# Graph attention with residual GCN: repeated rows by one load, two chunks in one load, and stores spread over steps

## The chip, the core and the metric

The kernel runs on one core of one Trainium2 chip. The metric is the device time of one execution in microseconds. A core has a matrix engine (PE; its weight loads are shown as PEld), a vector engine (DVE), an activation engine (ACT), a general engine (POOL) and a sync engine (SP) that does no arithmetic here and issues nearly all transfers. Sixteen DMA engines move the data of all queues between the chip's memory (HBM) and the on-chip memory, whose 128 rows are called partitions.

## The reference

Inputs are `x` (2708 x 128), a weighted adjacency matrix `adj` (2708 x 2708) and the weights of two layers.

```python
# layer 0: attention, h = 8 features a head, d = 128 heads, n = m = 2708 nodes
q = (x @ Wq.T).reshape(d, n, h)            # k and v alike
a = einsum('dnh,dmh->dnm', q, k) * d**-0.5 + adj + adj
o = einsum('dnm,dmh->dnh', softmax(a, axis=2), v).reshape(n, h * d) @ Wo.T
x = layernorm(x + o)
# layer 1: two graph convolutions and a residual
hid = adj @ (x @ W2) + b2
x = layernorm(x + adj @ (hid @ W4) + b4 + hid @ res_w.T + res_b)
```

Nearly all time goes into `a`: 128 heads of 2708 x 2708 scores, each of which gets the same `adj` added (twice), is exponentiated and multiplied with eight features and a column of ones.

## The kernel before

**Heads and blocks.** The 128 heads go in 32 groups of GB = 4. The 2708 queries go in 6 blocks of QB = 452 (the last of 448). The 2708 keys are 21 whole chunks of 128 (NU = 21) and a short one of 20. A block is worked through in nine steps, the list `plan`; 32 x 6 x 9 gives 1728 steps. Each step has two to four pieces, and a piece is two score tiles of 128 keys by 452 queries. PE makes the scores (`score`, L451), DVE adds the adjacency tile (`add_near`, L458), ACT takes the exponential of a whole step's tiles at once (L559), and PE multiplies with the values into `acc` (`add_up`, L476). For nine of the chunks (`TWO_EXP`), three heads of four go another way: ACT takes the exponential of the bare scores (L556) and POOL multiplies by the exponential of the adjacency tile (L557), which was stored in the first group (`near_exp`).

**Precision.** Keys and queries are split in a rounded part and a remainder. `qs` and `ks` in HBM have 16 rows: eight of the rounded parts, eight of the remainders. A score needs (k + k')(q + q'), so each head holds 32 partitions on chip: the keys as 8 rounded rows twice and then 8 remainder rows twice, the queries as all 16 rows twice.

**Loads.** All of these are issued by SP from within the step that is being written down, and they stand in SP's queue in that order.

- `load_adj(n)` (L303) issues the nth entry of `loads`, the adjacency tiles in the order of their use; there are 26 entries a block. An ordinary chunk is one load of 128 x 452 into `col` (L316), the stored exponential one into `ecol` (L312), and a piece made of two different chunks has two loads into the halves of one tile `two` (L309). They are issued in the first piece of a step (c == 0), up to `ahead` = 8 entries past what the step needs. There are 9 buffers of `col`, 3 of `two`, 7 of `ecol`.
- `load_keys(g + 1, h)` (L261) runs for h = 0 to 15, one call in every second of a group's first 32 steps (t counts a group's 54 steps). One call loads 8 rows of 2708 numbers into 8 partitions of `k_raw`. Later steps rearrange them on POOL (`order_keys`).
- `load_q` (L295) runs in step 3 of a block for the next block: eight loads in a row, each of 16 rows of 452 numbers.
- `hand_on` (L479) runs once a block: DVE copies `acc` to `o`, and SP issues four stores of 9 rows in a row (L485).
- In the first 27 groups there are also the projections of later rows: quarter by quarter a load of weights, a product, and stores to `qs`, `ks`, `vs`, as jobs taken out one at a time in the second piece of a step (c == 1).

**What sets the order.** `interleave` writes down the order of pieces, products and `hand_on` by a table of costs; it does not look at loads. Each engine then runs its own instructions in that order and waits on semaphores. The semaphores of SP's transfers are eight, used in turn, so that a ninth transfer waits until the first has landed.

**Before the loop** (L383 to L419) the first two chunks of rows are projected, stored to `ks`, `qs` and `vs`, and read back by sixteen `load_keys` and eight loads of `load_q`, alternating between SP's and ACT's queues. **After the loop** `finish` does the output projection, the layer norm and layer 1; in the last group some of its first inputs are loaded early.

Of the kernel before, what the change touches and what calls it, by code (L numbers as in the profile page):

```python
# [9 lines left out]
F32 = mybir.dt.float32  # L10
F32R = mybir.dt.float32r
# [7 lines left out]
P = 128  # L19
H = 8  # L20
GB = 4
NB = 512
QB = 452
# [12 lines left out]
def chunks(n, w):  # L36
    return [(i, min(w, n - i)) for i in range(0, n, w)]
# [102 lines left out]


@with_exitstack
def graph_attention_gcn(ctx: ExitStack, tc: tile.TileContext, x, xT, adj, adjT, adjP, adjS,
                        WqT, WkT, WvT, WoT, W2, b2, W4, b4, res_wT, res_b, out):


# [7 lines left out]
    nc = tc.nc  # L154
    N, D = x.shape
    R = N * D
    NG = D // GB
    MC = chunks(N, P)
    NM = len(MC)
    NBS = chunks(N, NB)  # L160
    QBS = chunks(N, QB)


    NU = NM - 1
# [14 lines left out]
    qs = dram.tile([2 * H, R], F32, name="qs")  # L179
    ks = dram.tile([2 * H, R], F32, name="ks")  # L180
    vs = dram.tile([R, H], F32, name="vs")
    os_ = dram.tile([H + 1, R], F32, name="os")
# [19 lines left out]
    with ExitStack() as s:  # L202
# [3 lines left out]
        qpool = s.enter_context(tc.tile_pool(name="qpool", bufs=2))  # L206
# [52 lines left out]
        groups, raw_keys, values, queries, adj_cols, exp_cols, acc = {}, {}, {}, {}, {}, {}, {}  # L259

        def load_keys(g, h, queue=nc.sync):  # L261


            if h == 0:
                groups[g] = kpool.tile([P, NU, P], F32R, tag="k", name="k"), k_short[g % 2], vals[g % 2], v_short[g % 2]
                raw_keys[g] = raw.tile([P, N], F32R, tag="k_raw", name="k_raw")
            queue.dma_start(raw_keys[g][ds(H * h, H), :].bitcast(F32),
                              ks[ds(H * (h % 4 // 2), H), ds((GB * g + h // 4) * N, N)])

        def order_keys(g, i, copy=nc.gpsimd.tensor_copy):  # L270

# [9 lines left out]
        def load_values(g, j):  # L281
            if j == 0:
                values[g] = raw.tile([P, GB, NU * H], F32, tag="v_raw", name="v_raw")
            vz = v_short[g % 2]
            r0 = (GB * g + j) * N
            nc.sync.dma_start(values[g][:, j, :], vs[ds(r0, P * NU), :].rearrange("(p c) e -> p (c e)", c=NU))
            nc.sync.dma_start(vz[ds(32 * j, SHORT), ds(32 * j, H)], vs[ds(r0 + P * NU, SHORT), :])

        def spread_values(g, j):
            to = vals[g % 2].rearrange("p c (j e) -> p j c e", e=VW)  # L290
            v = values[g][:, j, :].rearrange("p (c e) -> p c e", e=H)
            nc.gpsimd.tensor_copy(to[:, j, :, :H], v)
            nc.gpsimd.tensor_copy(v_first[g % 2][:, ds(32 * j, H)], v[:, first_chunk, :])

        def load_q(g, b, queues=(nc.sync, nc.sync)):  # L295
            n0, nw = QBS[b]
            q = queries[g, b] = qpool.tile([P, QB], F32R, tag="q", name="q")
            for j in range(GB):
                for i in range(2):
                    queues[i].dma_start(q[ds(32 * j + 2 * H * i, 2 * H), :nw].bitcast(F32),  # L300
                                      qs[:, ds((GB * g + j) * N + n0, nw)])

        def load_adj(n):  # L303
            g, b, m = loads[n]
            n0, nw = QBS[b]
            if isinstance(m, tuple):
                t = adj_cols[g, b, m] = twos.tile([P, 2, QB], F32, tag="two", name="two")
                for i, x in enumerate(m):
                    nc.sync.dma_start(t[:, i, :nw], (adjS if x == NU else adjP[ds(x * P, P), :])[:, ds(n0, nw)])  # L309
            elif m < 0 and g > 0:  # L310
                t = exp_cols[g, b, -1 - m] = ecols.tile([P, QB], F32, tag="ecol", name="ecol")
                nc.sync.dma_start(t[:, :nw], near_exp[b, -1 - m][:, :nw])  # L312
            else:
                t = adj_cols[g, b, m] = cols.tile([P, QB], F32, tag="col", name="col")
                m = -1 - m if m < 0 else m
                nc.sync.dma_start(t[:, :nw], adjP[ds(m * P, P), ds(n0, nw)])  # L316

        ahead = 8
        epool = s.enter_context(tc.tile_pool(name="weights", bufs=5))
# [88 lines left out]
        for i in range(2):  # L408
            project_all(0, i)()
        store_v = project_all(0, 2)  # L410
        for h in range(16):
            load_keys(0, h, nc.scalar if h % 2 else nc.sync)
        load_q(0, 0, (nc.sync, nc.scalar))
        store_v()
        for n in range(2, ahead):
            load_adj(n)
# [62 lines left out]
        def hand_on(g, b):  # L479
            n0, nw = QBS[b]  # L480
            o = opool.tile([P, QB], F32, tag="o", name="o")
            nc.vector.tensor_copy(o[:, :nw], acc.pop((g, b))[:, :nw])  # L482
            queue = nc.gpsimd if (g, b) == (NG - 1, len(QBS) - 1) else nc.sync
            for j in range(GB):
                queue.dma_start(os_[:, ds((GB * g + j) * N + n0, nw)], o[ds(32 * j, H + 1), :nw])  # L485

        where = {}

# [2 lines left out]
        for g in range(1, NG):  # L491
            c = (min(NG, g + 2) * GB * N - 1) // (P * P)
            assert c < FIRST or amid[quarters.index((c, 2, 3))] + 8 < 54 * g
        jobs = []
        loaded = ahead
        for what, n, c, beside in interleave(plan, len(steps) // len(plan), NU, amid, bufs=5):
            if what == "amid":
                at = amid.index(n)
                jobs += project(at)
                continue  # L500
            if what == "add_up":
                g, b = divmod(n, len(QBS))
                add_up(g, b, c, where.pop((g, b, c)))
                continue
            if what == "hand_on":
                hand_on(*divmod(n, len(QBS)))
                continue
            g, b, i = steps[n]
            pieces, two, _ = plan[i]
            nw = QBS[b][1]  # L510
            if c == 1 and jobs:
                jobs.pop(0)()
            if c == 0:
                nq = (g, b + 1) if b + 1 < len(QBS) else (g + 1, 0)
                if i == 3 and nq[0] < NG:
                    load_q(*nq)

                if g + 1 < NG:
                    t = b * len(plan) + i
                    if t < 32 and t % 2 == 0:  # L520
                        load_keys(g + 1, t // 2)
                    elif t < 32 and t % 8 == 7:
                        load_values(g + 1, t // 8)
                    elif 33 <= t < 50 and t % 2:
                        order_keys(g + 1, (t - 33) // 2)
                    elif t >= 50:
                        spread_values(g + 1, t - 50)
                if g == NG - 1 and i % 2 and early:
                    nc.sync.dma_start(*early.pop(0))
                last = max(loads.index((g, b, x), max(0, loaded - 40)) for x in [chunks_of(p) for p in pieces] + [-1 - two])  # L530
                while loaded < min(len(loads), last + 1 + ahead):
                    load_adj(loaded)
                    loaded += 1
                e = epool.tile([P, 8, QB], F32, tag="e", name="e")
                sp = pq.tile([P, 3, NB], F32, tag="p", name="p")
                w = ppool.tile([P, 3, QB], F32, tag="w", name="w")
                if g == 0:
                    first_exp(b, two)
                at = k = 0
            st = ps.tile([P, 2, NB], F32, tag="s", name="s")  # L540
            for r, (m, j) in enumerate(pieces[c]):
                score(st[:, r], g, b, m, j)
                where.setdefault((g, b, m), {})[j] = e, at + r
            for j in beside:
                score(sp[:, k], g, b, two, j)
                where.setdefault((g, b, two), {})[j] = w, k
                k += 1
            add_near(e, st, g, b, pieces[c], at)
            at += 2
            if c == len(pieces) - 1:  # L550
                look_at_near(g, b, two)
                if n == len(steps) - 1:
                    quotient = opool.tile([P, QB], F32, tag="o", name="o")[:, :P]
                    nc.vector.reciprocal(quotient, ot0[:, H, :])
                    nc.vector.tensor_mul(ot0[:, :H, :], ot0[:, :H, :], quotient.unsqueeze(1).to_broadcast([P, H, P]))
                nc.scalar.activation(w[:, :, :nw], sp[:, :, :nw], AF.Exp, scale=2.0)  # L556
                nc.gpsimd.tensor_mul(w[:, :, :nw], w[:, :, :nw],  # L557
                                     exp_cols[g, b, two][:, :nw].unsqueeze(1).to_broadcast([P, 3, nw]))
                nc.scalar.activation(e[:, :at, :nw], e[:, :at, :nw], AF.Exp, scale=2.0)  # L559
# [538 lines left out]
```

## Time and profile before

| what | value |
|---|---|
| median of the runs | 6857.9 us |
| range of the runs | 6836.81 to 6862.31 us |
| time of the profiled execution | 6849.71 us |
| its span | 6847.9 us |
| ACT busy | 6504.6 us (95%) |
| PE busy | 6633.7 us (97%) |
| DVE busy | 6117.5 us (89%) |
| POOL busy | 5791.3 us (85%) |
| DMA, mean busy share of 16 engines, SP's queue | 79.7% |
| moved | 1665.68 MB, 243 GB/s |

The shares are means over the whole span. The loop over steps runs from about 46 us to about 6536 us; the rest is the start and `finish`. A row of the window view gives each engine's busy time in one stretch, the number of its instructions, the granted clock, the DMA share and the rate. In a group's row the last part is idle time of the engine just before these instructions, and what ended most of it.

### The profile page before, as it was taken

To read this page: it belongs to the slowest core of one execution; us is meant where nothing else is said; L and a number is where in the kernel's file an instruction comes from. 1 tells how busy PE (TensorE), PEld (TensorE's weight loads), DVE (VectorE), ACT (ScalarE), POOL (GpSimd) and SP (SyncE) were. 2 spreads that over 40 slices of the span, in tenths; PEclk is the share of its full clock that TensorE was granted. 3 is DMA by queue.
4 is the path that set the end of the run, shared out by engine and by line. 5 is a ranking of instruction groups with operands and counts; after the bars stand their busy time and mean duration, and the time that the engine had idled before them with its cause. 6 is when DMAs were issued, how large, how long until landed. Compare 5 with 4: busy or idle time off the path is not lost.

```text
span 6847.9 us, 138426 instructions
## 1 busy us (share of the span) xinstructions
PE 6633.7 (97%) x50612; PEld 1982.5 (29%) x50612; DVE 6117.5 (89%) x6368; ACT 6504.6 (95%) x3660; POOL 5791.3 (85%) x2710
## 2 busy tenths in 40 slices
PE   7999999999999999999999999999999999999999
PEld 2222222222222222222222222222222222222254
DVE  5899999999999999999999999999999899999962
ACT  7999999999999999999999999999999999999930
POOL 5898988999988999989899989899998888888810
PEclk8999999999999999999999999999999999999999
DMA  8888888888888888888888888888888887777774
GB/s 244 265 248 249 254 251 242 250 245 244 248 248 253 245 250 250 251 245 249 244 245 249 248 253 252 251 241 249 247 245 240 233 242 233 234 234 235 233 262 131
DMA packets 1148664, 1665.68 MB, mean 243 GB/s; under 512 B 151560, under 2 KB 1130804, under 8 KB 1141300
## 3 DMA queue, kind: packets, MB, share of 16 engines
q1 hardware_dynamic: 1144808, 1654.51, 79.7%
q8 instruction: 401, 6.57, 0.4%
q10 hardware_dynamic: 3040, 2.19, 0.1%
q14 instruction: 287, 2.35, 0.1%
q0 software_dynamic: 128, 0.06, 0.0%
HBM read 1574.37 MB, written 81.80 MB: 242 GB/s over the span
## 4 chain that ended last, share of the span: by engine, by line
PE 46%; DMA 16%; DVE 9%; POOL 9%; issue 7%; SPq 7%; ACT 6%; DVEq 0%; POOLq 0%; ACTq 0%
PE acc L476 22%; PE s L451 14%; DVE e L458 8%; POOL w L557 8%; DMA col<-in_adjP 6%; SPq L300 4%; DMA two<-in_adjP 3%; ACT e L559 3%; DMA ecol<-ne 3%; ACT w L556 3%; PE acc L468 2%; PE acc L660 2%; PE acc L742 2%; PE p L451 1%; DMA k_raw<-ks 1%
## 5 line engine op out<-in xcount | busy, mean ns | idle before, releaser
L557 POOL TENSOR_TENSOR w<-w,ecol 128x1356 f32<-128x1356 f32 (+1 forms) x1728 | 5347.0, 3101 | 692.6 <-ACT w L556 615.7
L458 DVE TENSOR_TENSOR e<-s,col 128x904 f32<-128x904 f32 (+1 forms) x4608 | 4817.2, 1092 | 316.4 <-PE s L451 76.0
L559 ACT ACTIVATE e<-e 128x2712 f32<-128x2712 f32 (+5 forms) x1728 | 4635.5, 2683 | 19.3 <-DVE e L458 14.3
L476 PE MATMUL acc<-e,vals 128*9 128x452 f32 x20352 | 3564.0, 546 | 0.0
L451 PE MATMUL s<-q,k 32*128 32x452 f32 x10944 | 2495.0, 461 | 130.2 <-DVE e L458 95.5
L556 ACT ACTIVATE w<-p 128x1356 f32<-128x1356 f32 (+1 forms) x1728 | 2328.6, 1348 | 12.8 <-PE p L451 9.1
L451 PEld LDWEIGHTS s<-q,k 32*128 32x128 f32 x10944 | 1003.9, 182 | 3248.4 <-DVE e L458 2864.9
L476 PE MATMUL acc<-w,vals 128*9 128x452 f32 x10368 | 1627.4, 546 | 0.0
L451 PE MATMUL p<-q,k 32*128 32x452 f32 (+1 forms) x5184 | 1324.9, 445 | 21.8 <-ACT w L556 19.8
L458 DVE TENSOR_TENSOR e<-s,two 128x904 f32<-128x904 f32 (+1 forms) x960 | 1049.0, 1093 | 109.0 <-PE s L451 60.5
L476 PEld LDWEIGHTS acc<-e,vals 128*9 128x9 f32 x20352 | 442.3, 88 | 779.3 <-issue 778.1
L451 PEld LDWEIGHTS p<-q,k 32*128 32x128 f32 x5184 | 546.4, 182 | 50.5 <-ACT w L556 43.1
L476 PEld LDWEIGHTS acc<-w,vals 128*9 128x9 f32 x10368 | 209.9, 88 | 177.4 <-issue 161.0
L275 POOL CAST k<-k_raw 128x336 fp32r<-128x336 f32 x251 | 222.2, 885 | 35.9 <-DMA q<-qs 35.9
L473 PE MATMUL acc<-e,v_first 128*32 128x452 f32 (+1 forms) x1536 | 186.7, 558 | 12.7 <-ACT e L559 0.6
L468 PE MATMUL acc<-e,v_short 128*128 128x452 f32 (+1 forms) x384 | 196.7, 594 | 0.0
L357 PE MATMUL s<-wc,xc 128*128 128x256 f32 (+1 forms) x480 | 166.6, 429 | 4.7
L482 DVE COPY o<-acc 128x452 f32<-128x452 f32 x192 | 120.3, 627 | 46.1 <-PE acc L476 46.1
L359 DVE TENSOR_SCALAR pa<-s 128x256 f32<-128x256 f32 (+1 forms) x240 | 100.4, 418 | 31.6 <-PE s L357 23.7
L373 POOL TENSOR_TENSOR pr<-pa,pr 128x256 fp32r<-128x256 f32 (+1 forms) x160 | 117.5, 735 | 12.8
L357 PEld LDWEIGHTS s<-wc,xc 128*128 128x128 f32 (+1 forms) x480 | 69.6, 183 | 155.6 <-DVE e L458 152.5
L660 PE MATMUL acc<-rows,x 128*128 128x512 f32 (+2 forms) x252 | 105.1, 553 | 0.0
(91 smaller groups left out, 1029.5 us busy)
## 6 DMA issues: line engine op xcount, KB each, us to landing
col<-in_adjP SPq DMA_DIRECT2D x1965, 226.0 KB
two<-in_adjP SPq DMA_DIRECT2D x1440, 226.0 KB
ecol<-ne SPq DMA_DIRECT2D x1395, 226.0 KB
col<-in_adjP SPq DMA_DIRECT2D x393, 224.0 KB
two<-in_adjP SPq DMA_DIRECT2D x288, 224.0 KB
ecol<-ne SPq DMA_DIRECT2D x279, 224.0 KB
k_raw<-ks SPq DMA_DIRECT2D x504, 84.6 KB
two<-in_adjS SPq DMA_DIRECT2D x160, 226.0 KB
```

Of the source, the lines that this page charges most:

```text
L275: copy(k[:, :, ts(i, n)], t[:, ts(i, n * NU)].rearrange("p (q c) -> p c q", c=NU))
L300: queues[i].dma_start(q[ds(32 * j + 2 * H * i, 2 * H), :nw].bitcast(F32), qs[:, ds((GB * g + j) * N + n0, nw)])
L357: nc.tensor.matmul(pp[:mi, 0, :QW], given[c][:, :mi], given.pop((c, i, h)), start=True, stop=True)
L451: nc.tensor.matmul(to[:, :nw], k[r, m, :], q[r], start=True, stop=True)
L458: nc.vector.tensor_add(e[:, ds(at, 2), :nw], st[:, :, :nw], a)
L468: nc.tensor.matmul(a[:, :nw], vz, e[:, t, :nw], start=False, stop=False)
L473: nc.tensor.matmul(a[ds(32 * j, 32), :nw], v_first[g % 2][:, ds(32 * j, 32)], e[:, t, :nw], start=True, stop=False)
L476: nc.tensor.matmul(a[ds(32 * j, VW), :nw], v[:, m, ds(VW * j, VW)], e[:, t, :nw], start=False, stop=(m == last_chunk))
L556: nc.scalar.activation(w[:, :, :nw], sp[:, :, :nw], AF.Exp, scale=2.0)
L557: nc.gpsimd.tensor_mul(w[:, :, :nw], w[:, :, :nw], exp_cols[g, b, two][:, :nw].unsqueeze(1).to_broadcast([P, 3, nw]))
L559: nc.scalar.activation(e[:, :at, :nw], e[:, :at, :nw], AF.Exp, scale=2.0)
L660: nc.tensor.matmul(accs[k][:, :nw], x1[:mw, m, :], rows[m][:mw, ds(n0, nw)], start=(m == 0), stop=(m == NM - 1))
```

## The change

Four things are edited. Keys: a call of `load_keys` now loads 16 partitions, 8 rows of `ks` that the load reads twice (`to_broadcast`), so that a group has eight calls in place of sixteen, one in every fourth step. Queries: a call of `load_q` loads one head's 32 partitions, the 16 rows of `qs` read twice; the four calls stand in steps 3 to 6 of a block. Adjacency: the short chunk is put in front of `adjP` in HBM, so that two chunks of a `two` tile are one load with a step between them. Stores: `hand_on` returns its four stores, and one is issued in the second piece of each of the following steps; those of the last block are issued at once.

As built, the access patterns of a key load are 16 rows by 2708 on chip and, in HBM, 2 (step 0) by 8 by 2708; of a query load 32 by 452 on chip and 2 (step 0) by 16 by 452 in HBM; of a `two` load 128 by 2 by 452 on both sides. No instruction of PE, DVE, ACT or POOL in the loop is added or removed.

```diff
         def load_keys(g, h, queue=nc.sync):
...
-            queue.dma_start(raw_keys[g][ds(H * h, H), :].bitcast(F32),
-                              ks[ds(H * (h % 4 // 2), H), ds((GB * g + h // 4) * N, N)])
+            part = ks[ds(H * (h % 2), H), ds((GB * g + h // 2) * N, N)]
+            queue.dma_start(raw_keys[g][ds(2 * H * h, 2 * H), :].bitcast(F32), part.unsqueeze(0).to_broadcast([2, H, N]))
...
-        def load_q(g, b, queues=(nc.sync, nc.sync)):
+        def load_q(g, b, j, queue=nc.sync):
             n0, nw = QBS[b]
-            q = queries[g, b] = qpool.tile([P, QB], F32R, tag="q", name="q")
-            for j in range(GB):
-                for i in range(2):
-                    queues[i].dma_start(q[ds(32 * j + 2 * H * i, 2 * H), :nw].bitcast(F32),
-                                      qs[:, ds((GB * g + j) * N + n0, nw)])
+            if j == 0:
+                queries[g, b] = qpool.tile([P, QB], F32R, tag="q", name="q")
+            part = qs[:, ds((GB * g + j) * N + n0, nw)]
+            queue.dma_start(queries[g, b][ds(32 * j, 32), :nw].bitcast(F32), part.unsqueeze(0).to_broadcast([2, 2 * H, nw]))
+
+        chunk_rows = adjP.rearrange("(c p) n -> p c n", p=P)
...
                 t = adj_cols[g, b, m] = twos.tile([P, 2, QB], F32, tag="two", name="two")
-                for i, x in enumerate(m):
-                    nc.sync.dma_start(t[:, i, :nw], (adjS if x == NU else adjP[ds(x * P, P), :])[:, ds(n0, nw)])
+                x, x1 = ((i + 1) % NM for i in m)
+                nc.sync.dma_start(t[:, :, :nw], chunk_rows[:, ds(x, 2, step=x1 - x), ds(n0, nw)])
...
-        for h in range(16):
+        for h in range(8):
             load_keys(0, h, nc.scalar if h % 2 else nc.sync)
-        load_q(0, 0, (nc.sync, nc.scalar))
+        for j in range(GB):
+            load_q(0, 0, j, nc.scalar if j % 2 else nc.sync)
...
-            queue = nc.gpsimd if (g, b) == (NG - 1, len(QBS) - 1) else nc.sync
-            for j in range(GB):
-                queue.dma_start(os_[:, ds((GB * g + j) * N + n0, nw)], o[ds(32 * j, H + 1), :nw])
+            last = (g, b) == (NG - 1, len(QBS) - 1)
+
+            def store(j):
+                (nc.gpsimd if last else nc.sync).dma_start(os_[:, ds((GB * g + j) * N + n0, nw)], o[ds(32 * j, H + 1), :nw])
+
+            stores = [lambda j=j: store(j) for j in range(GB)]
+            while last and stores:
+                stores.pop(0)()
+            return stores
...
             if c == 1 and jobs:
                 jobs.pop(0)()
+            if c == 1 and sums:
+                sums.pop(0)()
             if c == 0:
                 nq = (g, b + 1) if b + 1 < len(QBS) else (g + 1, 0)
-                if i == 3 and nq[0] < NG:
-                    load_q(*nq)
+                if 3 <= i < 3 + GB and nq[0] < NG:
+                    load_q(*nq, i - 3)
...
-                    if t < 32 and t % 2 == 0:
-                        load_keys(g + 1, t // 2)
+                    if t < 32 and t % 4 == 0:
+                        load_keys(g + 1, t // 4)
...
-        "adjP": adj.T[: n // P * P].reshape(P, n // P, n).transpose(1, 0, 2).reshape(n // P * P, n),
-        "adjS": adj_short,
+        "adjP": np.concatenate([adj_short, adj.T[: n // P * P].reshape(P, n // P, n).transpose(1, 0, 2).reshape(-1, n)]),
```

More of the change, by code (lines that the diff above doesn't have):

```diff
@@ L142, in graph_attention_gcn @@
 @with_exitstack
-def graph_attention_gcn(ctx: ExitStack, tc: tile.TileContext, x, xT, adj, adjT, adjP, adjS,
+def graph_attention_gcn(ctx: ExitStack, tc: tile.TileContext, x, xT, adj, adjT, adjP,
                         WqT, WkT, WvT, WoT, W2, b2, W4, b4, res_wT, res_b, out):
@@ L315, in load_adj @@
                 m = -1 - m if m < 0 else m
-                nc.sync.dma_start(t[:, :nw], adjP[ds(m * P, P), ds(n0, nw)])
+                nc.sync.dma_start(t[:, :nw], chunk_rows[:, m + 1, ds(n0, nw)])
         ahead = 8
@@ L493, in graph_attention_gcn @@
             assert c < FIRST or amid[quarters.index((c, 2, 3))] + 8 < 54 * g
-        jobs = []
+        jobs, sums = [], []
         loaded = ahead
@@ L505, in graph_attention_gcn @@
             if what == "hand_on":
-                hand_on(*divmod(n, len(QBS)))
+                sums += hand_on(*divmod(n, len(QBS)))
                 continue
```

## The prediction

> **What bounds the kernel now.** I read the page first, then the windows, to see whether its shares hold in the loop; then who waited for whom; then SP's own waits, because the change only touches SP's transfers; last the DMA view and, underneath it, the trace's records of packets and semaphore updates.
>
> The page:
>
> ```profile
> span 6847.9 us, 138426 instructions
> PE 6633.7 (97%) x50612; PEld 1982.5 (29%) x50612; DVE 6117.5 (89%) x6368; ACT 6504.6 (95%) x3660; POOL 5791.3 (85%) x2710
> DMA  8888888888888888888888888888888887777774
> q1 hardware_dynamic: 1144808, 1654.51, 79.7%
> L458 DVE TENSOR_TENSOR e<-s,col 128x904 f32<-128x904 f32 (+1 forms) x4608 | 4817.2, 1092 | 316.4 <-PE s L451 76.0
> L559 ACT ACTIVATE e<-e 128x2712 f32<-128x2712 f32 (+5 forms) x1728 | 4635.5, 2683 | 19.3 <-DVE e L458 14.3
> L556 ACT ACTIVATE w<-p 128x1356 f32<-128x1356 f32 (+1 forms) x1728 | 2328.6, 1348 | 12.8 <-PE p L451 9.1
> ```
>
> Stretches of the loop:
>
> ```profile
> 50.00:1000.00 950.00, 913.25 (x6980) 261.25 (x6983) 850.11 (x855) 939.00 (x595) 820.92 (x389) 0.98 0.85 255
> 2000.00:3000.00 1000.00, 980.55 (x7682) 279.63 (x7679) 927.15 (x938) 995.85 (x537) 903.87 (x431) 1.00 0.82 248
> 5000.00:6000.00 1000.00, 974.40 (x7612) 283.39 (x7608) 920.89 (x920) 992.77 (x535) 883.46 (x394) 0.99 0.79 238
> 6500.00:6848.00 348.00, 329.67 (x1494) 176.38 (x1492) 153.65 (x346) 78.36 (x105) 36.79 (x21) 0.97 0.59 195
> ```
>
> The sixth number is ACT: 995.85 of 1000. With the stretches not shown, ACT is busy 6414.7 of the 6450 us from 50 to 6500, and its two groups idle 19.3 + 12.8 us in the whole run. ACT is the bound, and **35 us is all that better feeding can save in the loop**. The number before the last is the DMA share, 0.82: the second resource, with 18% left if the load is spread evenly over 16 engines.
>
> SP's waits, and who waits for transfers now:
>
> ```profile
> SPq L485 <- DVE o L482: 438.6, 166, 8.8
> SPq L309 <- DMA two<-in_adjP: 134.8, 393, 1.8
> SPq L312 <- DMA col<-in_adjP: 126.0, 341, 1.7
> ...
> DVE e L458 <- DMA two<-in_adjP: 20.4, 22, 3.4
> DVE e L458 <- DMA col<-in_adjP: 10.8, 19, 3.8
> ```
>
> SP stands 438.6 us at the stores of a block's sums, and then issues eight query loads. Yet DVE waits only 20.4 + 10.8 us for tiles. Matching each tile's landing with its first use in the trace gives why: at the median a `col` lands 6.5 us before its use, a `two` 7.0, an `ecol` 8.3; only the tiles behind the query burst are near (2.0 to 2.7 us).
>
> The start, in the chain:
>
> ```profile
> 20.56 10.22 DMA k_raw<-ks
> 30.80 9.77 DMA k_raw<-ks
> 40.58 0.31 SPq L300
> ```
>
> **The change, part by part.** The step is 6490 us of loop / 1728 = 3.76 us, a group 202.8, its 32 steps with key loads 120.2, the other 22 steps 82.6.
>
> *Two chunks in one load, and the short chunk in front.* 1920 loads become 960 of twice the size. The same rows reach the same partitions; 16 rows an engine in place of 2 x 8. The second half was issued 0.45 us after the first and DVE needs both, so the landing hardly moves. It removes 960 x 0.40 us of SP's issuing, which lies beside ACT. Cost 0.
>
> *Stores in four steps.* They go behind the job of the same second piece, and past the tile loads of the next steps. By then the copy `o` (0.63 us) is long done, so the 438.6 us wait of SP goes. What SP now meets first is a semaphore that is still out, a landing (rows of 134.8 and 126.0 above). Nobody waits for the stores before `finish`; the last block's are issued as before. Cost 0.
>
> *Query burst gone.* Eight issues of 0.43 us in a row become four, a step apart, each past about three tile loads. The tiles behind them, now 2.0 to 2.7 us early, come as early as the others. The last of the four is issued in step 6, needed two steps (7.5 us) later at the earliest. What all this can return is between 0 and the 35 us of ACT's idling; I take 10, since DVE's waits for tiles (31 us) are only partly behind the burst.
>
> *Repeated rows: where they run.* This decides. In the trace's semaphore records every DMA tells how many engines it used: a load of 128 or of 16 rows raises its semaphore in 16 updates; every 8-row key load (504 of 504 on SP) in nine, one at about 0.5 us and then eight; every 9-row store in ten, one and nine; every 20-row one in eleven, one and ten. So a DMA is cut into equal parts along its outermost count, at most 16, and 20 rows make 10. The parts of few go to the same engines: at 32.07 us, behind the first key loads, a 16-row query load had eight updates after 1.57 to 1.67 us and eight after 8.30 to 8.70. Nothing in this trace has different outermost counts on its two sides. The new loads do: 16 or 32 on chip, 2 in HBM. The bounds are 16 engines (cut by the rows on chip) and 2 (cut so that both sides come out equal). I take 2: all counts seen are divisors of the outermost count, and a part must be a part on both sides.
>
> The page "DMA: Bandwidth & Descriptors" of the Trainium skill (section "Why a DMA increments its semaphore by 16 and not by 1", and the rules for authors) says the same in general: the count is the largest up to 16 that divides the slowest dimension of both patterns, on the lowest-numbered engines, and a leading zero-stride repeat "confines the whole DMA to at most c engines". The counts 16, 10, 9 and 8 of this trace agree with it; for a repeat no run here shows it. By the page the sum below stands; by the on-chip rows alone it would be the first rival's.
>
> *What two engines must then carry, per group.* From the packet records of the loop: a row of 1808 B takes 95.3 ns in the mean, 75 at the tenth percentile, 87.4 when no key packet is within 2 us; a key row of 10,832 B takes 611 ns in the mean, 519 in the median, 407 at the tenth percentile; in `finish`, where 16 engines each load rows of that size for their own partitions, 448.
>
> - All else now: 0.82 x 202.8 = 166.3 us an engine, less keys 128 x 611 / 16 = 4.9 and queries 768 x 95.3 / 16 = 4.6: 156.8. With key traffic on two engines only, I scale by 87.4 / 95.3: 143.8, or 0.709 of the time.
> - Keys: 64 rows each. Two engines write at once where eight did, so between 448 and 519; I take 475: 30.4 us, all within the 120.2.
> - Queries: 384 rows x 87.4 = 33.6 us, 19.9 within the 120.2.
>
> In the steps with key loads: 85.2 + 30.4 + 19.9 = 135.5 us of work in 120.2, 15.3 too much. In the others: 58.6 + 13.7 = 72.3 of 82.6, 10.3 to spare. Every tile has rows on these two engines, so every tile is late by the backlog. About 8 us of it is covered by tiles landing early (6.5 to 8.3 now, and no burst), and the spare 10.3 pays that back in time for the next group. The rest, 7.3 us, stops DVE and then ACT: **31 x 7.3 = 226 us**.
>
> Ends: with every row at its shortest, 73.1 + 26.0 + 17.1 = 116.2, which fits: 0. With today's means for all, 92.9 + 39.1 + 21.7 = 153.7, 33.5 too much, of which 3.8 is paid back: 29.7 x 31 = 921.
>
> *The start.* Sixteen key loads end at 40.6 us, the queries at 42.2. Now each of two engines has 64 key rows (26.0 to 39.1 us by the same durations) and 64 query rows (4.8 to 6.1) from 17.4 us on (15.96 and 1.4 for the first landing): the end is at 48.2 to 62.6, 6 to 20 later, with the first scores waiting. At 475 ns and 87.4 ns it is 12 later, and nothing covers it.
>
> *Sum.* 6849.7 (the profiled time: span and 1.8 around it) + 226 + 12 - 10 = 7078. The profiled execution is 8 us under the median of the runs; with that, 7085.
>
> **Rivals.**
>
> 1. *The repeat is cut by the on-chip rows: 16 engines.* Not slower. For it: no repeat is in this trace. Against: see above. Price: keys and queries stay as spread as now, the start has half as many key loads to issue (perhaps 10 less), the loop returns 0 to 35: 6813 to 6850. The turning point, from the same terms: 85.2 + (60.8 + 39.8) / c fits 120.2 from three engines, so four would do.
> 2. *Two engines, but they keep up.* If the crowding in today's means comes from key traffic and goes with it, rows may fall to 75 to 80 ns. With keys at 407 the excess is covered by the 8 us up to 85 ns a row. Then only the start counts: 6850 to 6880.
> 3. *SP's eight semaphores.* A key load now takes 8 x 475 = 3.8 us on its engine, on top of a backlog, and the ninth transfer after any unlanded one waits. SP issues 35 in a block of 33.8 us (45.7 before, projections aside), so it needs landings within 7.7 us in the mean. If backlogged key loads land at 9.7, each of 248 holds SP by 2 us more, up to 496: about 7350. It worsens the forecast and shows as SP waits on landings.
>
> **How the numbers follow.** Two engines and late tiles 0.73 (rival 3 included, 0.12); two engines that keep up 0.13; sixteen engines 0.14. The median shown varies by under 0.4%, and 0.5% is about what a measurement of this kernel tells from no change. Rival 1 would be faster than that (under 6824) in 0.05 of its 0.14. Rival 2 lies within 0.5%, up to 6892, nearly always (0.12). Faster 0.05, same 0.21, slower 0.74. The range goes from inside rival 1, 6840, to above rival 3, 7420; 0.08 is left below and 0.11 above, where the 921 lies. The likeliest case alone has 6930 to 7350.
>
> **What would show it.** Right: a key load raises its semaphore in three updates (one, then two) and a query load likewise; packet counts are otherwise as now; the mean DMA share falls while `e<-s,col`, `e<-s,two` and the POOL product wait on DMA landings, hundreds of us in all, in the 32 steps with key loads and not in the others; ACT falls below 97% in the loop; the first scores start at 52 to 66 us. Wrong: sixteen updates and ACT still at 995 of 1000 (rival 1); three updates, waits on landings under 40 us (rival 2). SP's wait at the stores should be near zero in any case. My number fails if the row durations on two crowded engines are not those of today: each 5 ns on a 1808 B row is about 6 us a group, 190 us in all.

## The result and the profile after

The changed kernel takes 7202.6 us in the median (7199.8 to 7211.8), the kernel before 6850.3 in the same comparison: a ratio of 1.0522, 95% interval 1.0505 to 1.0539. The prediction had 7078, or 7085 by the median of the runs known then, in a range of 6840 to 7420. The profiled execution has a span of 7210.0 us, 362.1 more than before.

The page of the changed kernel (its lines are numbered a little higher: the scores are L453, DVE's addition L460, ACT's two exponentials L569 and L566, POOL's product L567):

```profile
span 7210.0 us, 135800 instructions
PE 6778.5 (94%) x50612; PEld 1992.7 (28%) x50612; DVE 6118.1 (85%) x6368; ACT 6527.6 (91%) x3660; POOL 5790.2 (80%) x2710
q1 hardware_dynamic: 1102940, 1654.35, 76.2%
L460 DVE TENSOR_TENSOR e<-s,col 128x904 f32<-128x904 f32 (+1 forms) x4608 | 4814.4, 1091 | 491.4 <-PE s L453 147.0
L569 ACT ACTIVATE e<-e 128x2712 f32<-128x2712 f32 (+5 forms) x1728 | 4585.8, 2654 | 96.9 <-DVE e L460 91.0
L566 ACT ACTIVATE w<-p 128x1356 f32<-128x1356 f32 (+1 forms) x1728 | 2278.6, 1319 | 256.3 <-PE p L453 137.3
```

DVE's 6118 and POOL's 5790 us are those of before. ACT is busy for 23 us more, PE for 145 us more (6778.5 against 6633.7), of which more below. ACT is idle before its two groups for 96.9 + 256.3 us, where it was 19.3 + 12.8. The bytes are the same, in fewer packets.

The same stretches as before, by windows:

```profile
50.00:1000.00 950.00, 870.06 (x6482) 245.10 (x6486) 792.87 (x798) 879.29 (x567) 764.90 (x367) 0.95 0.80 239
2000.00:3000.00 1000.00, 949.79 (x7230) 266.84 (x7232) 872.95 (x884) 942.51 (x506) 845.95 (x398) 0.97 0.78 233
5000.00:6000.00 1000.00, 951.19 (x7277) 269.41 (x7277) 879.01 (x884) 949.36 (x510) 849.29 (x395) 0.97 0.77 230
```

ACT has 942.5 of 1000 us where it had 995.9, and the DMA engines' mean share went *down*, from 0.82 to 0.78, while engines wait for transfers. The three longest of these waits:

```profile
POOL w L567 <- DMA ecol<-ne: 136.5, 77, 4.3
DVE e L460 <- DMA col<-in_adjP: 105.4, 42, 8.6
DVE e L460 <- DMA two<-in_adjP: 86.3, 41, 5.4
```

and where SP stands, by the four longest rows of key landings and the row of the stores:

```profile
SPq L310 <- DMA k_raw<-ks: 332.0, 76, 5.7
SPq L317 <- DMA k_raw<-ks: 287.4, 71, 5.7
SPq L313 <- DMA k_raw<-ks: 247.5, 49, 5.8
SPq L488 <- DVE o L484: 205.8, 73, 6.8
SPq L378 <- DMA k_raw<-ks: 83.8, 19, 5.5
```

In these four rows SP waits 950.7 us at key loads that have not landed; in the kernel before the longest such row has 54.0 us.

**Where the 362 us lie.** From the ends of POOL's 1728 products in the two traces: the first product ends 9.5 us later (54.5 to 64.1 us), the way from the first to the last is 356.8 longer (6487.4 to 6844.2), the rest is 4.3 shorter. Mean length of a step in groups 1 to 30, in us, by the step's number in its group:

| steps | 0-7 | 8-15 | 16-23 | 24-31 | 32-39 | 40-46 | 47-53 | group |
|---|---|---|---|---|---|---|---|---|
| before | 3.62 | 3.78 | 3.64 | 3.86 | 3.81 | 3.76 | 3.67 | 201.5 |
| after | 3.62 | 3.80 | 4.21 | 4.54 | 3.95 | 3.75 | 3.67 | 212.7 |

The loss is 10.1 us in the 32 steps with key loads (nearly all of it in the second half of them), 1.1 in the other 22.

**PE's clock.** In the steps that lose time PE's granted clock falls. Three stretches of one group of the changed kernel; the first lies in its first 16 steps, the others between step 14 and step 31:

```profile
2890.00:2935.00 45.00, 44.19 (x350) 12.80 (x346) 41.41 (x43) 44.93 (x25) 38.22 (x13) 1.00 0.70 209
2935.00:2975.00 40.00, 36.36 (x260) 9.92 (x260) 32.08 (x34) 33.99 (x19) 28.16 (x10) 0.91 0.81 219
2975.00:3010.00 35.00, 31.01 (x227) 8.30 (x223) 26.60 (x29) 30.00 (x17) 26.39 (x13) 0.90 0.83 225
```

PE takes 0.126 us a matmul in the first (44.19 for 350) and 0.140 in the second. By the clock records the granted clock is half for 436 us of the loop, where it was 46 before, and 372 of these 436 lie in steps 16 to 31 of groups 1 to 30. The 145 us that PE works longer come with this. PE is busy for 980.55 of 1000 us before and has little to spare, so this can lengthen a stall that a late tile began. How much of the loss it makes is not shown.

**Two engines.** In the semaphore records every key load (252 of 252 on SP, 4 of 4 on ACT) and every query load (766 and 2) now has three updates, one and then two. Loads of 128 rows still have sixteen, but the last two come late: a `col` load issued in steps 8 to 31 has its 14th update after 3.9 us in the median and 6.4 at the ninetieth percentile, its 16th after 5.4 and 10.2 (before: 4.4 and 5.6; 5.1 and 6.1). Fourteen engines are done, two are not.

Share of the time with so many data packets of SP's queue in flight on the DMA engines, groups 1 to 30, counted from the packet records:

| kernel, steps | none | one | two or three | 14 or more |
|---|---|---|---|---|
| before, 16-23 | 0.025 | 0.021 | 0.037 | 0.723 |
| after, 8-15 | 0.000 | 0.002 | 0.176 | 0.573 |
| after, 16-23 | 0.000 | 0.003 | 0.124 | 0.650 |
| after, 24-31 | 0.000 | 0.003 | 0.134 | 0.637 |
| after, 32-39 | 0.112 | 0.013 | 0.022 | 0.694 |

In steps 8 to 31 the share without a packet rounds to 0.000, and in an eighth of the time or more there are only two or three. The packet records do not name the engine, but this is what two engines that work without a break make while the others stand still. After the last key load the idle instants are back. The mean share of 16 engines (0.78) does not show this.

### The profile page after: what moved, and what is told of

Its sections match the earlier page's. It is cut to its first block, busy times and chain, and to the rows that moved or that the text cites. A ratio compares the mean times of both kernels' runs of the same rounds, so it can differ in the third digit from the quotient of the medians.

```text
span 7210.0 us, 135800 instructions
## 1 busy us (share of the span) xinstructions
PE 6778.5 (94%) x50612; PEld 1992.7 (28%) x50612; DVE 6118.1 (85%) x6368; ACT 6527.6 (91%) x3660; POOL 5790.2 (80%) x2710
## 4 chain that ended last, share of the span: by engine, by line
PE 45%; DMA 29%; DVE 10%; issue 6%; ACT 4%; POOL 4%; SPq 2%; DVEq 0%; ACTq 0%; POOLq 0%
PE acc L478 22%; PE s L453 14%; DVE e L460 9%; DMA col<-in_adjP 9%; DMA two<-in_adjP 7%; DMA ecol<-ne 4%; DMA q<-qs 4%; POOL w L567 3%; DMA k_raw<-ks 3%; ACT w L566 2%; ACT e L569 2%; PE acc L670 1%; PE acc L752 1%; PE p L453 1%; PE acc L470 1%
## 5 line engine op out<-in xcount | busy, mean ns | idle before, releaser
L567 POOL TENSOR_TENSOR w<-w,ecol 128x1356 f32<-128x1356 f32 (+1 forms) x1728 | 5345.7, 3099 | 1050.5 <-ACT w L566 798.8
L460 DVE TENSOR_TENSOR e<-s,col 128x904 f32<-128x904 f32 (+1 forms) x4608 | 4814.4, 1091 | 491.4 <-PE s L453 147.0
L569 ACT ACTIVATE e<-e 128x2712 f32<-128x2712 f32 (+5 forms) x1728 | 4585.8, 2654 | 96.9 <-DVE e L460 91.0
L478 PE MATMUL acc<-e,vals 128*9 128x452 f32 x20352 | 3673.2, 562 | 0.0
L453 PE MATMUL s<-q,k 32*128 32x452 f32 x10944 | 2525.6, 469 | 312.2 <-DVE e L460 264.8
L566 ACT ACTIVATE w<-p 128x1356 f32<-128x1356 f32 (+1 forms) x1728 | 2278.6, 1319 | 256.3 <-PE p L453 137.3
L453 PEld LDWEIGHTS s<-q,k 32*128 32x128 f32 x10944 | 1014.9, 185 | 3529.5 <-DVE e L460 3101.1
L478 PE MATMUL acc<-w,vals 128*9 128x452 f32 x10368 | 1670.0, 559 | 0.0
L453 PE MATMUL p<-q,k 32*128 32x452 f32 (+1 forms) x5184 | 1344.0, 449 | 25.2 <-ACT w L566 24.3
L460 DVE TENSOR_TENSOR e<-s,two 128x904 f32<-128x904 f32 (+1 forms) x960 | 1047.9, 1092 | 216.7 <-DMA two<-in_adjP 82.5
L453 PEld LDWEIGHTS p<-q,k 32*128 32x128 f32 x5184 | 555.2, 184 | 48.4 <-ACT w L566 41.7
L374 POOL TENSOR_TENSOR pr<-pa,pr 128x256 fp32r<-128x256 f32 (+1 forms) x160 | 117.5, 734 | 12.8
```

The lines of the kernel that those rows point to most:

```text
L453: nc.tensor.matmul(to[:, :nw], k[r, m, :], q[r], start=True, stop=True)
L460: nc.vector.tensor_add(e[:, ds(at, 2), :nw], st[:, :, :nw], a)
L478: nc.tensor.matmul(a[ds(32 * j, VW), :nw], v[:, m, ds(VW * j, VW)], e[:, t, :nw], start=False, stop=(m == last_chunk))
L567: nc.gpsimd.tensor_mul(w[:, :, :nw], w[:, :, :nw], exp_cols[g, b, two][:, :nw].unsqueeze(1).to_broadcast([P, 3, nw]))
```

## The experiments

Three theories. A: the two engines have more work in these steps than time; what binds is the sum of it. B: a key load on two engines lands late, and through the eight semaphores holds SP, which then issues everything late; each such load costs its hold. C: the loss comes from another part (merged tiles, spread stores, the repeat itself).

### Only the queries on two engines

```diff
-            part = ks[ds(H * (h % 2), H), ds((GB * g + h // 2) * N, N)]
-            queue.dma_start(raw_keys[g][ds(2 * H * h, 2 * H), :].bitcast(F32), part.unsqueeze(0).to_broadcast([2, H, N]))
+            queue.dma_start(raw_keys[g][ds(H * h, H), :].bitcast(F32),
+                              ks[ds(H * (h % 4 // 2), H), ds((GB * g + h // 4) * N, N)])
...
-                    if t < 32 and t % 4 == 0:
-                        load_keys(g + 1, t // 4)
+                    if t < 32 and t % 2 == 0:
+                        load_keys(g + 1, t // 2)
```

> The changed kernel with its key loads as before (sixteen of 8 rows a group), everything else changed: of the repeated loads only the queries remain on two engines. Theory A (the two engines have more work than time): in the 32 steps with key loads 85.2 us of all else, about 5 of keys and 19.9 of queries make 110 of 120.2, which fits; 6830 to 6865. Theory B (a key load on two engines lands late and, through the eight semaphores, holds SP): no such key load is left, so also 6830 to 6865. Theory C (the loss lies in the merged tiles or the spread stores): near 7200.

Measured: 6830.9 us, ratio to the kernel before 0.9984 (0.9974 to 0.9993). Theory C is out for the merged tiles and the spread stores, and queries on two engines alone cost nothing.

### Only the keys on two engines

```diff
-            queue.dma_start(queries[g, b][ds(32 * j, 32), :nw].bitcast(F32), part.unsqueeze(0).to_broadcast([2, 2 * H, nw]))
+            for i in range(2):
+                queue.dma_start(queries[g, b][ds(32 * j + 2 * H * i, 2 * H), :nw].bitcast(F32), part)
```

> The changed kernel with its query loads as before in shape (two of 16 rows a head, so eight a block, still spread over four steps): only the keys remain on two engines. Theory A: with the 634 ns a key row that the changed kernel's trace has, 85.2 + 40.6 + 2.7 = 128.5 us in 120.2, 8.3 too much, of which about 8 is covered by tiles that land early; only the start and little more is lost: 6855 to 6960. Theory B: the key loads are those of the changed kernel, with its 950 us of SP waiting for their landing, so most of the loss stays: 7100 to 7200. Theory C: near 7200.

Measured: 7051.1 us, ratio 1.0312 (1.0295 to 1.0329). It lies between what A and B expected, so it decides nothing alone: A's sum, with 8 us of cover, was too low, and B's too high. SP's waits at key landings are nearly those of the changed kernel (836.7 us in these four lines against 950.7), though the loss is little more than half:

```profile
SPq L318 <- DMA k_raw<-ks: 345.8, 90, 5.7
SPq L311 <- DMA k_raw<-ks: 211.2, 51, 5.1
SPq L314 <- DMA k_raw<-ks: 169.4, 41, 5.7
SPq L301 <- DMA k_raw<-ks: 110.3, 21, 11.7
```

### Neither on two engines

Both edits above together.

> The changed kernel with key and query loads both as before in shape; merged tiles, spread query calls and spread stores are left. Theories A and B: no loss, and what the smoother queue of SP returns of ACT's idle 35 us: 6815 to 6850. Theory C: near 7200.

Measured: 6831.1 us, ratio 0.9985 (0.9975 to 0.9994). So on top of this, queries alone cost nothing, keys alone about 0.033 of the time (1.0312 less 0.9985) and both 0.054 (1.0522 less 0.9985): the queries cost 0.021 when the keys are there and nothing when they are not. That is what a sum against a limit would do. PE's time at half clock in the loop grows in the same way (25 us with neither, 29 with the queries, 246 with the keys, 436 with both), so part of the growth may be PE's.

### The same loads, in an order that spreads them

```diff
-            part = ks[ds(H * (h % 2), H), ds((GB * g + h // 2) * N, N)]
-            queue.dma_start(raw_keys[g][ds(2 * H * h, 2 * H), :].bitcast(F32), part.unsqueeze(0).to_broadcast([2, H, N]))
+            part = ks[:, ds((GB * g + h // 2) * N, N)].rearrange("(l r) n -> r l n", l=2)
+            queue.dma_start(raw_keys[g][ds(2 * H * h, 2 * H), :].bitcast(F32), part)
...
-            queue.dma_start(queries[g, b][ds(32 * j, 32), :nw].bitcast(F32), part.unsqueeze(0).to_broadcast([2, 2 * H, nw]))
+            queue.dma_start(queries[g, b][ds(32 * j, 32), :nw].bitcast(F32), part.unsqueeze(1).to_broadcast([2 * H, 2, nw]))
```

A score is a sum over 32 rows, so their order is free as long as keys and queries have the same. Here a query row stands twice in succession, and against it the rounded and the remainder row of the key.

> The changed kernel with the same number and size of loads, but the 32 rows of a head in another order on both sides: each query row twice in succession (16 rows outermost, the repeat inside), and the keys as 8 rows outermost with rounded part and remainder inside, so that the same products are summed. Theories A and B: a query load raises its semaphore in sixteen updates and a key load in nine (one and eight); 6810 to 6850. If the number of engines is not the cause (the repeat itself, or loads of twice the size): near 7200.

Measured: **6815.6 us, ratio 0.9961 (0.9947 to 0.9975)**, faster than both kernels. The semaphore records have nine updates for every key load and sixteen for every query load. The number and the size of the loads and the repeat of the query rows are those of the changed kernel; the outermost count differs. A key load here also has 16 different rows, where it had 8 rows twice. That repeat did not slow the rows: a key row takes 715 ns in the mean here and 634 in the changed kernel. Its window, and its two ACT groups:

```profile
2000.00:3000.00 1000.00, 983.54 (x7695) 282.62 (x7696) 928.49 (x941) 998.34 (x538) 905.09 (x430) 1.00 0.81 249
```

```profile
L569 ACT ACTIVATE e<-e 128x2712 f32<-128x2712 f32 (+5 forms) x1728 | 4620.9, 2674 | 7.6 <-DVE e L460 1.3
L566 ACT ACTIVATE w<-p 128x1356 f32<-128x1356 f32 (+1 forms) x1728 | 2314.3, 1339 | 6.6 <-PE s L453 4.4
```

ACT stands at 998 of 1000; there is nothing more to save by feeding it. The first scores start at 34.6 us, before at 45.7.

### Key loads issued by ACT

```diff
-                        load_keys(g + 1, t // 4)
+                        load_keys(g + 1, t // 4, nc.scalar)
```

> The changed kernel with the loop's key loads (eight a group, two engines each) issued by ACT in place of SP; nothing else differs. Theory A (the two engines have more work than time, whoever issues): they stay as full, 7190 to 7280, with up to 159 us of ACT's own issuing (248 loads of 0.64 us) partly inside the stalls. Theory B (the loss is SP standing at a semaphore of a key load that has not landed): SP's 950 us of waits on key landings vanish and the loss with them; what is left is ACT's issuing, near 7000.

Measured: 7241.9 us, ratio 1.0589 (1.0571 to 1.0606). SP's waits at key landings:

```profile
SPq L300 <- DMA k_raw<-ks: 60.9, 26, 14.4
SPq L313 <- DMA k_raw<-ks: 56.0, 14, 4.3
SPq L310 <- DMA k_raw<-ks: 26.4, 7, 5.2
SPq L287 <- DMA k_raw<-ks: 16.5, 13, 2.1
```

The four longest are 159.8 us in all where they were 950.7, and the kernel is not faster, as theory A expected. But the run does not put theory B out, because the hold moved along: ACT now stands at the key loads that it issues, until an earlier transfer has landed. The changed kernel has no such rows before this exponential, which reads none of these tiles:

```profile
ACT w L566 <- DMA ecol<-ne: 88.4, 15, 8.1
ACT w L566 <- DMA col<-in_adjP: 70.2, 13, 6.6
ACT w L566 <- DMA os<-o: 43.9, 12, 5.6
```

These 202.5 us and 156 us of issuing (252 x 0.62) are together about as much as the whole loss, though the run is only some 46 us (0.0067 of the time) slower than the changed kernel. What speaks against B as a price for each held load is elsewhere: keys alone have nearly the same waits of SP with little more than half of the loss, the next run has half of the waits with a fifth of the loss, and in the changed kernel there is no instant without a packet in steps 8 to 31, so no gap is seen that issuing sooner could fill. A and B are also not apart in one respect: SP stands because the key loads land late. What the loss would be if SP never stood was not tried.

### Half of the key rows

```diff
-            queue.dma_start(raw_keys[g][ds(2 * H * h, 2 * H), :].bitcast(F32), part.unsqueeze(0).to_broadcast([2, H, N]))
+            if h % 2 == 0:
+                queue.dma_start(raw_keys[g][ds(2 * H * h, 2 * H), :].bitcast(F32), part.unsqueeze(0).to_broadcast([2, H, N]))
+            else:
+                for i in range(2):
+                    queue.dma_start(raw_keys[g][ds(2 * H * h + H * i, H), :].bitcast(F32), part)
```

> The changed kernel with every second key load (the remainders) as two loads of 8 rows on eight engines again: half the key rows are on two engines, the queries all. Theory A, a threshold: 20.3 us of key rows on two engines, about 2.5 of the others, 19.9 of queries and 71 to 85 of all else make 114 to 128 in 120.2, which fits or is covered by tiles that land early: 6830 to 6880. Theory B, so much for each key load that lands late: half of the loss, 6990 to 7040.

Measured: 6892.4 us, ratio 1.0082 (1.0065 to 1.0099): 0.0097 over the kernel with neither, where half of 0.0537 would be 0.027. A part of it is the start (first scores at 59.7 us); a group of 54 steps takes 202.7 us against 201.1 with neither. So half of the key rows cost 1.6 us a group and all of them 11.6: a threshold, as A says, though 12 us over the range that A gave. SP's four longest waits at key landings are half of the changed kernel's (479.6 us against 950.7), the loss is less than a fifth:

```profile
SPq L317 <- DMA k_raw<-ks: 160.5, 40, 5.7
SPq L314 <- DMA k_raw<-ks: 151.4, 65, 5.6
SPq L321 <- DMA k_raw<-ks: 118.4, 94, 5.3
SPq L382 <- DMA k_raw<-ks: 49.3, 18, 4.2
```

The instants without a packet in steps 16 to 31 are still 0.000, which fits two engines that are just full.

### Four engines

On the turned order, keys by sixteen loads a group with 4 rows outermost:

```diff
-            part = ks[:, ds((GB * g + h // 2) * N, N)].rearrange("(l r) n -> r l n", l=2)
-            queue.dma_start(raw_keys[g][ds(2 * H * h, 2 * H), :].bitcast(F32), part)
+            part = ks[:, ds((GB * g + h // 4) * N, N)].rearrange("(l r) n -> r l n", l=2)
+            queue.dma_start(raw_keys[g][ds(H * h, H), :].bitcast(F32), part[ds(4 * (h % 2), 4)])
```

with sixteen calls for the keys, in the start and in the loop, as in the first experiment.

> The order of rows with the repeat inside, but keys as sixteen loads of 8 partitions a group, 4 rows of ks outermost: five semaphore updates (one and four), so four engines; queries on sixteen. Theory A: 20.3 us of key rows on each of four engines, 85.2 of all else and 2 of queries make 108 in 120.2: no loss in the loop, 6810 to 6850. If the loss went with the number of engines without a threshold, half of what keys alone lost on two: near 6940.

Measured: 6818.6 us, ratio 0.9968 (0.9957 to 0.9978). No loss on four engines.

### What the other two parts are worth

With the turned order kept, once the tiles of two chunks by two loads again, once the stores and the query loads in a row again:

```diff
-                nc.sync.dma_start(t[:, :, :nw], chunk_rows[:, ds(x, 2, step=x1 - x), ds(n0, nw)])
+                for i, x in enumerate((x, x1)):
+                    nc.sync.dma_start(t[:, i, :nw], chunk_rows[:, x, ds(n0, nw)])
```

> The turned order of rows (key loads on eight engines, query loads on sixteen), but each tile of two chunks again by two loads. Of the 25 us that the turned order was under the kernel before, about 11 are the start (first scores at 34.6 us in place of 45.7). If the merged load is worth nothing in the loop, as the prediction had it: the same as the turned order within 5 us, 6811 to 6821. If SP's 960 issues of 0.40 us count: 6825 to 6840.

```diff
-            while last and stores:
+            while stores:
...
-                if 3 <= i < 3 + GB and nq[0] < NG:
-                    load_q(*nq, i - 3)
+                if i == 3 and nq[0] < NG:
+                    for j in range(GB):
+                        load_q(*nq, j)
```

> The turned order and the merged load, but the four stores of a block in a row as before, and the four query loads in a row in step 3. If the spread of both is what returns some of ACT's idle 35 us (I took 10): 6822 to 6832. If it is worth nothing: 6811 to 6821.

Measured: 6812.5 and 6815.8 us, 0.9964 (0.9951 to 0.9978) and 0.9968 (0.9956 to 0.9980) of the kernel before, against 0.9961 for the turned order with both. Neither part is worth anything that can be measured here once the loads are fewer and spread.

## Why the prediction was right, and what it had mis-sized

- **ACT as the bound, at most 35 us to gain: right.** The turned kernel has ACT at 998.3 of 1000 and is 0.9961 of the time, 27 us, part of it at the start, outside that ceiling.
- **Where the rows run: right, and it decided.** It was inferred from divisors in the trace of before, and three updates on every load of both kinds show it; the turned order, with eight and sixteen engines, has no loss. The rule of the Trainium skill that was named ("DMA: Bandwidth & Descriptors", section "Why a DMA increments its semaphore by 16 and not by 1") gives all counts seen here: 2 for both repeats, 4, 8 and 16 in the experiments.
- **The place: right.** The loss is in the steps with key loads. The first half of these is as before (3.62 and 3.80 us a step), which fits tiles that landed early and cover the backlog at first, and the steps after them are nearly as before.
- **The size: the term of the late tiles was mis-sized, 226 us against about 347** (11.2 a group x 31). The step that failed is the key row at 475 ns, taken in the belief that two writers are quicker than eight. It measured 634 in the mean over the loop, above the 611 of before. That alone adds 159 ns x 64 = 10.2 us a group and would have given 25.5 too much, less 8 of cover, 17.5 x 31 = 542. So the other terms were too high by some 6 us a group, in the rows of 1808 B on these engines (at instants with at most three packets their median is 75 ns, their mean 92.5) or in how the cover was counted. The packet records do not name the engine, so how these two share it stays open. The sum also has no term for PE's clock, whose share in the 347 us is not known. The errors partly cancelled: with the mean of all engines for the short rows too (96 ns measured, 87.4 taken) the same sum gives about 1000 us. That 226 lies as near to 347 as it does is in part luck.
- **The start: right in kind.** First scores at 52.1 us, at the lower edge of the 52 to 66 given; 6.4 later than before, 9.5 by the first product, against 12.
- **Merged load 0: right. Return of 10 us by the smoother queue: the size was right, the reason was not shown.** With neither repeat the kernel is 0.9985 of the time, 10 us. But a row of four queries and four stores costs nothing measurable in the turned kernel. The row of eight query loads that the kernel before has was not tried by itself.
- **SP's wait at the stores near zero: wrong.** It is 205.8 us here and 366.7 in the turned kernel, which is among the fastest: SP arrives there ahead of DVE, and nothing behind it is late. A long wait of a queue that is ahead is no cost.
- **Rivals.** The sixteen engines (rival 1) did not happen by themselves, but its price holds where they were made to: 6815.6 lies in its 6813 to 6850, and its turning point below four engines agrees with the run on four. Two engines that keep up (rival 2) is what the queries alone are; its key row at 407 ns did not come. SP's semaphores (rival 3) show in the waits as described: key loads issued in steps 8 to 31 land after 10.0 us in the median, and SP's hold is 950.7 us where up to 496 was allowed. A price for each held load does not fit the runs with keys alone and with half of the keys; a part in the loss is not excluded.

## What to carry to other kernels

A load that repeats rows should have the repeat inside and the rows outside: the outermost count of both sides decides over how many DMA engines it runs, and here 2 in place of 8 or 16 cost 5.4% at a mean DMA share that looked harmless. Where every tile is spread over all engines, judge the load on the fullest engine, over the steps in which it is fullest, and look at the number of semaphore updates per load to learn the count. If a sum like this runs over only when two parts come together, testing the parts one at a time understates each of them.

## What was not expected of the hardware

A row of 10,832 B takes 407 ns at the tenth percentile before the change, but in the loop often about twice that: with two engines carrying the keys, the upper quarter of these rows is at 814 ns and more when 14 or more packets are in flight. Their median is then 674 ns, and 418 when at most three are in flight; but in the kernel before the few rows with at most three have 704, so other traffic alone does not set a row's time. With eight engines (the turned order) the mean is even 715 ns, and it costs nothing there: the share of time without a packet of SP's queue is 0.07 to 0.09 in steps 8 to 31. What the rows share with the other traffic was not tried.

The granted clock of PE over the profiled execution was 0.966 in the changed kernel, 0.993 before and 0.996 in the turned one. In steps 24 to 31 a matmul `acc<-e,vals` takes 625 ns in the mean where it was 547, and 545 again in steps 32 to 39. So late transfers came together with a slower PE in the same steps. Whether the lower clock adds to the loss was not tried.
